# A graph-attention kernel in 64x64 array tiles: part of each softmax denominator summed on VectorE

## The chip, the cores and the metric

The kernel runs on one core of one Trainium2 chip. The metric is the device time of one execution in microseconds (us). The kernel before was run three times: 2678.79, 2678.89 and 2681.78 us, median 2678.89. The profiled execution took 2678.89 us; its span, from the first to the last recorded instruction, is 2677.1 us.

## The reference

One graph-attention layer with four heads, a second one with a single head on its output, then two layer normalisations with a residual. There are 8 batch entries, 2048 nodes and 64 features.

```python
mask = graph + eye(N) > 0                       # 2048 x 2048
h = einsum('bnc,hdc->bhnd', x, Wh)              # four heads of 64
# gat(h): scores = h h^T; where not mask: -1e16; softmax over m; times h; plus bias
z = leaky_relu(concat_heads(gat(h)), 0.2)
h2 = einsum('bnk,dk->bnd', z, Wo)
z2 = leaky_relu(gat(h2), 0.2)
out = layernorm(x + (layernorm(z2) * gamma + beta))
```

The softmax needs, for every query node, the sum over all 2048 nodes m of exp(score). These sums, the denominators, are what the change is about.

## The kernel before, in words

All times come from `fast_kernel`; `general_kernel` runs only if the range check at the end asks for it.

**Units, chunks, blocks.** A unit is a pair of maps that are worked on together, one on partitions 0 to 63 and one on 64 to 127: two heads of one batch entry (a first-layer unit, 16 in all), or the second layer of two batch entries (a second-layer unit, 4 in all). The units are numbered 0 to 19 in the order of the list `order`; 5, 10, 18 and 19 are of the second layer. A unit has 4 chunks of 512 query nodes, a chunk 16 blocks of 128 nodes m: 1280 steps, each one block of one chunk.

**One step** t. TensorE makes the scores of its block (`scores`, L537: 4 products in 64x64 array tiles, of which float32 makes 8 instructions) into one of two PSUM buffers "s" of 128x1024. VectorE subtracts the mask from them and writes the block's tile e, 128x1024 float32, to SBUF (L540). ScalarE takes the exponential in place (L541). Three steps later (`LAG`) TensorE multiplies e by the values (`values`, L550: again 8 instructions), and `add_up` deals with the denominator. On TensorE a step is thus scores of block t, then values of block t-3. The next scores but one need the same "s" buffer, so they wait for the subtraction.

**The denominator.** Before, blocks 1 to 12 of a first-layer chunk (1 to 8 in the second layer) are added into acc by GpSimd, one addition of 128x1024 each (L559 the first, L563 the others). The last blocks, 3 or 7 by `DIRECT`, stay as they are. With acc that makes 4 or 8 terms. `sums` (L597) has TensorE multiply each half of the terms by ones, in 128x32 tiles, four at a time: 2 or 4 groups of 8 instructions. The result goes by ScalarE (L600) and small DMAs to `invert` (L613, L615), which inverts it and sends it back by DMA, spread over partitions; `scale` (L624) multiplies.

**Order.** Every engine works its instructions in the order in which they are written. Jobs hang on a chunk's first step t (`LATE`, `NORM`): join at t+19, join2 (VectorE, L577) and sums at t+20, fifth t+21, leaky (VectorE, L585) t+22, invert t+24, scale t+28, project (TensorE, L641 in odd chunks of the second pair of heads, L631 in every second-layer chunk) t+30. A chunk's jobs from t+16 on so run among the blocks of the next chunk: "step 4 of the next chunk" is t+20. In the last chunk of a unit, steps 1 and 6 prepare the next unit (`prepare`: 8 transposes, L527, into an "s" buffer, which VectorE copies with an addition, L529). `NORM` are the second layer's normalisation parts from t+31 to t+46, on ScalarE, VectorE and GpSimd: at t+43 GpSimd takes a power (L694), which ScalarE needs at t+46 (L698). In the first 60 steps the byte mask is built beside the work.

**Buffers.** The tiles e, and raw pieces of adj and x, share 13 buffers of 4 KB ("e", `epool`); results of 512 columns share 6 ("w", `work`).

Of the kernel before, what the change touches and what calls it, by code (L numbers as in the profile page):

```python
# [24 lines left out]
F32 = mybir.dt.float32  # L29
# [4 lines left out]
OP = mybir.AluOpType  # L34
AX = mybir.AxisListType
# [320 lines left out]
def fast_kernel(ctx: ExitStack, tc: tile.TileContext, x, adj, Wh, bh, Wo, bo, gamma, beta, out, flag):  # L356

    nc = tc.nc
    B, N, C = x.shape
    H, D, _ = Wh.shape  # L360
    P = 128
    NB = N // P
    W = 512
# [2 lines left out]
    HP = H // 2  # L366
    K = 2 * CB
    LAG = 3
    DIRECT = (3, 7)

    const = ctx.enter_context(tc.tile_pool(name="const", bufs=1))
    big = ctx.enter_context(tc.tile_pool(name="big", bufs=2))
    epool = ctx.enter_context(tc.tile_pool(name="epool", bufs=13))
    accs = ctx.enter_context(tc.tile_pool(name="accs", bufs=2))
    work = ctx.enter_context(tc.tile_pool(name="work", bufs=6))
    small = ctx.enter_context(tc.tile_pool(name="small", bufs=4))
    psum = ctx.enter_context(tc.tile_pool(name="psum", bufs=2, space=bass.MemoryType.PSUM))
    dram = ctx.enter_context(tc.tile_pool(name="scratch", bufs=4, space=bass.MemoryType.DRAM))
# [1 line left out]
    def slot(shape, dtype, name):  # L380
        return epool.tile(shape, dtype, tag="e", name=name)

    def spsum(name, dtype=F32):
        n = 2 * W * 4 // mybir.dt.size(dtype)
        return psum.tile([P, n], dtype, tag="s", name=name)
# [4 lines left out]
    def wtile(name):  # L390
        return work.tile([P, W], F32, tag="w", name=name)
# [13 lines left out]
    for r in range(2):  # L405
        half = centre[r * D:(r + 1) * D, r, :]
        nc.vector.tensor_scalar(half, half, -1.0 / D, None, OP.add)
    ones = const.tile([P, 32], F32, name="ones")
# [20 lines left out]
    def load_x(bp):  # L429
        sts = []  # L430
        for h in range(2):
            st = slot([P, NB // 2, 2, C], F32, f"x{bp}_{h}")
            for b2 in range(2):
                nc.sync.dma_start(out=st[:, :, b2, :],
                                  in_=x[2 * bp + b2, h * N // 2:(h + 1) * N // 2].rearrange("(c p) d -> p c d", p=P))
            sts.append(st)
        return sts

    def transpose_x(bp, sts, h):
        if h == 0:  # L440
            xT[bp] = big.tile([P, N], F32, tag="xT", name=f"xT{bp}", bufs=1)
        p = spsum(f"px{bp}_{h}")
        for k in range(NB // 2):
            nc.tensor.transpose(p[:, k * P:(k + 1) * P], sts[h][:, k].rearrange("p b d -> p (b d)"), ident)
        nc.scalar.copy(xT[bp][:, h * 1024:(h + 1) * 1024], p)
# [52 lines left out]
    def project_x(bp, hp, q):  # L498

        if q == 0:  # L500
            maps[bp, hp] = big.tile([P, 2, N], F32, tag="hT", name=f"hT{bp}_{hp}")
        p = spsum(f"ph{bp}_{hp}_{q}").rearrange("p (b i) -> p b i", b=2)
        for b2 in range(2):
            rows = slice(b2 * C, (b2 + 1) * C)
            for j in range(2):
                nc.tensor.matmul(p[j * D:(j + 1) * D, b2, :], whT[rows, hp * P + j * D:hp * P + (j + 1) * D],
                                 xT[bp][rows, q * W:(q + 1) * W], start=True, stop=True)
        nc.scalar.copy(maps[bp, hp][:, :, q * W:(q + 1) * W], p)  # L508

    class Unit:  # L510
# [21 lines left out]
        def scores(self, c, m):  # L532
            ps = spsum(f"s{self.n}_{c}_{m}").rearrange("p (j i) -> p j i", j=2)
            for k in range(2):
                for j in range(2):
                    rows = slice(j * D, (j + 1) * D)
                    nc.tensor.matmul(ps[k * 64:(k + 1) * 64, j, :], self.hT[rows, m * P + k * 64:m * P + (k + 1) * 64],  # L537
                                     self.hT[rows, c * W:(c + 1) * W], start=True, stop=True)
            e = slot([P, 2, W], F32, f"e{self.n}_{c}_{m}")
            nc.vector.tensor_tensor(e, ps, mask[c][:, m, :].unsqueeze(1).to_broadcast([P, 2, W]), OP.subtract)  # L540
            nc.scalar.activation(e, e, AF.Exp, bias=shifts[:, 1:2] if self.second else shifts[:, 0:1], scale=1.0)  # L541
            return e
# [10 lines left out]
        def add_up(self, c, m, e):  # L553

            if m == 0:
                self.terms[c] = [e]
            elif m == 1:
                acc = accs.tile([P, 2, W], F32, tag="acc", name=f"acc{self.n}_{c}")
                nc.gpsimd.tensor_tensor(acc, self.terms[c][0], e, OP.add)  # L559
                self.terms[c] = [acc]  # L560
            elif m < NB - DIRECT[self.second]:
                acc = self.terms[c][0]
                nc.gpsimd.tensor_tensor(acc, acc, e, OP.add)  # L563
            else:
                self.terms[c].append(e)


        def join(self, c):
# [18 lines left out]
        def sums(self, c):  # L587

            n = self.n
            pz = spsum(f"pz{n}_{c}")  # L590
            terms = self.terms.pop(c)
            half = len(terms) // 2
            for k in range(half):
                for s in range(2):
                    for j in range(2):
                        q = (2 * s + j) * 32
                        nc.tensor.matmul(pz[q:q + 32, :W], ones, terms[s * half + k][:, j, :],  # L597
                                         start=(k == 0), stop=(k == half - 1), tile_position=(0, q))
            zsb = wtile(f"zsb{n}_{c}")
            nc.scalar.copy(zsb, pz[:, :W])  # L600
            zt = small.tile([P, 2, 8], F32, tag="zt", name=f"zt{n}_{c}")
            with nc.allow_non_contiguous_dma(reason="2 KB"):
                for s in range(2):
                    for j in range(2):
                        q = (2 * s + j) * 32
                        nc.sync.dma_start(out=zt[j * D:(j + 1) * D, s, :],
                                          in_=zsb[q:q + 1, :].rearrange("o (p k) -> o p k", k=8))
            self.zt[c] = zt

        def invert(self, c):  # L610
            n = self.n
            k = n * NC + c
            nc.vector.tensor_reduce(zall[:, k, :], self.zt.pop(c).rearrange("p s k -> p k s"), AX.X, OP.add)  # L613
            rt = small.tile([P, 8], F32, tag="rt", name=f"rt{n}_{c}")
            nc.vector.reciprocal(rt, zall[:, k, :])  # L615
            rd = dram.tile([2, W], F32, tag="rd", name=f"rd{n}_{c}")
            nc.sync.dma_start(out=rd.rearrange("j (p k) -> (j p) k", k=8), in_=rt)
            self.z[c] = wtile(f"z{n}_{c}")
            for j in range(2):
                nc.sync.dma_start(out=self.z[c][j * D:(j + 1) * D, :], in_=rd[j].partition_broadcast(D))  # L620

# [98 lines left out]
    def at(t, job):  # L720
        jobs.setdefault(t, []).append(job)
# [36 lines left out]
    for t in range(total + 64):  # L758
        if t < total:
            u, c, m = steps[t]  # L760
            es[t] = u.scores(c, m)
            if m == 0:
                for d, name in LATE:
                    at(t + d, lambda u=u, c=c, name=name: getattr(u, name)(c))
                for part, d in enumerate(NORM):
                    at(t + d, lambda u=u, c=c, part=part: u.norm(c, part))

                n = u.n + 1
                if n < len(units):
                    v = units[n]  # L770
                    lead = not v.second and v.b2 == 0
                    if lead and v.hp == 0:
                        if c == 0:
                            xst[v.bp] = load_x(v.bp)
                        elif c == 1:
                            for h in range(2):
                                at(t + 2 + 4 * h, lambda v=v, h=h: transpose_x(v.bp, xst[v.bp], h))
                    if lead and c == 2:
                        for q in range(NC):
                            at(t + 1 + 3 * q, lambda v=v, q=q: project_x(v.bp, v.hp, q))  # L780
                    if c == 3:
                        for h in range(2):
                            at(t + 1 + 5 * h, lambda v=v, h=h: v.prepare(h))
        if 0 <= t - LAG < total:
            u, c, m = steps[t - LAG]
            e = es.pop(t - LAG)
            u.values(c, m, e)
            u.add_up(c, m, e)
        for job in jobs.pop(t, ()):
            job()  # L790
# [53 lines left out]
```

## Time and profile before

| | |
|---|---|
| median of 3 runs | 2678.89 us |
| profiled execution | 2678.89 us, its span 2677.1 us |
| TensorE matmul busy | 2580.8 us (96%), 23174 instructions |
| VectorE busy | 1832.5 us (68%) |
| ScalarE busy | 1783.3 us (67%) |
| GpSimd busy | 2265.1 us (85%) |
| granted TensorE clock | 0.985 in the mean |
| scores L537, values L550 | 20480 matmul instructions of the 23174 |
| denominators on TensorE, L597 | 1536 matmul instructions |
| denominators on GpSimd, L559 and L563 | 896 additions of some 2.37 us |

In the page, PE is TensorE, DVE VectorE, ACT ScalarE, POOL GpSimd, SP the engine that issues most DMAs; L540 is line 540 of the kernel. Matmuls overlap, so a group of 8 that is listed with 1.04 us is followed by the next group 0.86 us after its start; where the distance matters, starts are compared and not durations. An idle time stands beside the engine's instruction that came after it, with what released it.

### The profile page before, as it was taken

To read this page: it belongs to the slowest core of one execution; us is meant where nothing else is said; L and a number is where in the kernel's file an instruction comes from. 1 tells how busy PE (TensorE), PEld (TensorE's weight loads), DVE (VectorE), ACT (ScalarE), POOL (GpSimd) and SP (SyncE) were. 2 spreads that over 40 slices of the span, in tenths; PEclk is the share of its full clock that TensorE was granted. 3 is DMA by queue.
4 is the path that set the end of the run, shared out by engine and by line. 5 is a ranking of instruction groups with operands and counts; after the bars stand their busy time and mean duration, and the time that the engine had idled before them with its cause. 6 is when DMAs were issued, how large, how long until landed. Compare 5 with 4: busy or idle time off the path is not lost.

```text
span 2677.1 us, 54824 instructions
## 1 busy us (share of the span) xinstructions
PE 2580.8 (96%) x23174; PEld 896.5 (33%) x23174; DVE 1832.5 (68%) x1797; ACT 1783.3 (67%) x2089; POOL 2265.1 (85%) x1041
## 2 busy tenths in 40 slices
PE   7999999999999999999999899999999999999993
PEld 3333333333333233333333233333333333333331
DVE  5876776677766577667776667767776777766662
ACT  5766666666667666666667766666666666666774
POOL 5889999899688999889967989988998999967774
PEclk9999999999999999999999999999999999999996
DMA  5300001000001001000001000100000000000011
GB/s 143 125 25 10 9 9 25 10 14 10 13 17 25 9 14 25 10 10 10 10 14 25 21 9 10 25 9 14 9 9 10 10 10 13 10 13 17 21 25 29
DMA packets 118304, 55.40 MB, mean 21 GB/s; under 512 B 91266, under 2 KB 107714, under 8 KB 118050
## 3 DMA queue, kind: packets, MB, share of 16 engines
q1 hardware_dynamic: 117250, 51.36, 7.2%
q8 instruction: 183, 3.00, 0.5%
q0 software_dynamic: 176, 0.26, 0.1%
q14 instruction: 71, 0.58, 0.1%
q10 hardware_dynamic: 624, 0.20, 0.0%
HBM read 46.60 MB, written 4.52 MB: 19 GB/s over the span
## 4 chain that ended last, share of the span: by engine, by line
PE 76%; POOL 11%; ACT 6%; DVE 3%; issue 3%; DMA 0%; SPq 0%; POOLq 0%; DVEq 0%; ACTq 0%
PE s L537 34%; PE o L550 33%; POOL acc L563 6%; PE pz L597 5%; ACT e L541 3%; DVE e L540 2%; PE pn L527 1%; ACT xr L698 1%; PE o L641 1%; ACT xr L690 1%; POOL acc L559 1%; POOL st L694 1%; POOL st L679 1%; ACT hT L508 1%; PE pm L484 1%
## 5 line engine op out<-in xcount | busy, mean ns | idle before, releaser
L540 DVE TENSOR_TENSOR e<-s,mask 128x1024 f32<-128x1024 f32 x1280 | 1562.6, 1222 | 721.7 <-PE s L537 700.3
L563 POOL TENSOR_TENSOR acc<-acc,e 128x1024 f32<-128x1024 f32 x816 | 1933.5, 2369 | 81.2 <-ACT e L541 20.2
L541 ACT ACTIVATE e<-e,shifts 128x1024 f32<-128x1024 f32 x1280 | 1465.1, 1148 | 762.5 <-DVE e L540 748.4
L550 PE MATMUL o<-e,hN 64*64 64x512 f32 x10240 | 1336.6, 592 | 20.2 <-ACT e L541 20.1
L537 PE MATMUL s<-hT 64*64 64x512 f32 x8192 | 1074.3, 595 | 9.6 <-DVE e L540 4.5
L550 PEld LDWEIGHTS o<-e,hN 64*64 64x64 f32 x10240 | 390.9, 134 | 738.6 <-issue 540.7
L537 PEld LDWEIGHTS s<-hT 64*64 64x64 f32 x8192 | 295.8, 133 | 582.2 <-issue 424.9
L559 POOL TENSOR_TENSOR acc<-e,e 128x1024 f32<-128x1024 f32 x80 | 189.3, 2367 | 139.5 <-ACT e L541 139.2
L537 PE MATMUL s<-h2T 64*64 64x512 f32 x2048 | 273.1, 604 | 15.7 <-DVE e L540 15.6
L597 PE MATMUL pz<-e,ones 128*32 128x512 f32 x1216 | 182.1, 600 | 0.0
L679 POOL TENSOR_TENSOR st<-st,mhalf 128x8 f32<-128x8 f32 x16 | 26.3, 1641 | 127.3 <-ACT st L678 127.3
L537 PEld LDWEIGHTS s<-h2T 64*64 64x64 f32 x2048 | 75.2, 135 | 157.9 <-issue 121.3
L597 PE MATMUL pz<-acc,ones 128*32 128x512 f32 x320 | 85.0, 610 | 0.1
L600 ACT COPY zsb<-pz 128x512 f32<-128x512 f32 x80 | 46.7, 584 | 48.3 <-PE pz L597 48.3
L698 ACT ACTIVATE xr<-y,st 128x64 f32<-128x64 f32 x128 | 44.1, 426 | 42.8 <-POOL st L695 42.8
L597 PEld LDWEIGHTS pz<-e,ones 128*32 128x32 f32 x1216 | 41.0, 110 | 68.5 <-issue 68.5
L585 DVE TENSOR_TENSOR o<-o,o 128x512 f32<-128x512 f32 x80 | 55.8, 698 | 5.2 <-ACT o L581 5.2
L624 DVE TENSOR_TENSOR z<-o,z 128x512 f32<-128x512 f32 x80 | 54.5, 681 | 6.0 <-DMA z<-rd 5.7
L577 DVE TENSOR_TENSOR o<-o,oj 128x512 f32<-128x512 f32 x80 | 55.9, 698 | 2.4 <-ACT oj L572 1.0
L485 DVE CAST mask<-pm 128x1024 uint8<-128x1024 bf16 x32 | 39.1, 1223 | 18.5 <-PE pm L484 16.6
L581 ACT ACTIVATE o<-o 128x512 f32<-128x512 f32 x80 | 46.2, 577 | 0.0
L572 ACT COPY oj<-o 128x512 f32<-128x512 f32 x80 | 45.6, 569 | 0.4
(74 smaller groups left out, 681.8 us busy)
## 6 DMA issues: line engine op xcount, KB each, us to landing
z<-rd SPq DMA_DIRECT2D x160, 128.0 KB, 2.9
adj<-in_adj_dram SPq DMA_DIRECT2D x32, 512.0 KB, 4.8
zt<-zsb SPq DMA_DIRECT2D x320, 2.0 KB, 1.8
x<-in_x_dram SPq DMA_DIRECT2D x16, 256.0 KB, 4.6
xr<-in_x_dram SPq DMA_DIRECT2D x32, 128.0 KB, 2.7
out_dram<-xr SPq DMA_DIRECT2D x32, 128.0 KB, 2.1
rd<-rt SPq DMA_DIRECT2D x80, 4.0 KB, 1.4
ws<-in_L_gnn_Wh_dram ACTq DMA_DIRECT2D x2, 64.0 KB, 4.6
```

The source lines that it names most:

```text
L537: nc.tensor.matmul(ps[k * 64:(k + 1) * 64, j, :], self.hT[rows, m * P + k * 64:m * P + (k + 1) * 64], self.hT[rows, c * W:(c + 1) * W], st ...
L540: nc.vector.tensor_tensor(e, ps, mask[c][:, m, :].unsqueeze(1).to_broadcast([P, 2, W]), OP.subtract)
L541: nc.scalar.activation(e, e, AF.Exp, bias=shifts[:, 1:2] if self.second else shifts[:, 0:1], scale=1.0)
L550: nc.tensor.matmul(self.O[c][r][j * D:(j + 1) * D, :], self.hN[rows, m, j * D:(j + 1) * D], e[rows, j, :], start=(m == 0), stop=(m == NB - 1))
L559: nc.gpsimd.tensor_tensor(acc, self.terms[c][0], e, OP.add)
L563: nc.gpsimd.tensor_tensor(acc, acc, e, OP.add)
L577: nc.vector.tensor_tensor(b, b, self.t, OP.add)
L585: nc.vector.tensor_tensor(b, b, self.t, OP.max)
L597: nc.tensor.matmul(pz[q:q + 32, :W], ones, terms[s * half + k][:, j, :], start=(k == 0), stop=(k == half - 1), tile_position=(0, q))
L624: nc.vector.tensor_tensor(dst, self.O[c][1], self.z[c], OP.mult)
L679: nc.gpsimd.tensor_tensor(st[:, 0, :], st[:, 1, :], mhalf, OP.pow)
L698: nc.scalar.activation(v(xr)[:, k, :], v(y)[:, k, :], AF.Identity, bias=st[:, 1, k:k + 1], scale=st[:, 0, k:k + 1])
```

## The change

Blocks 2, 4, 6 and 8 of every chunk are written into one tile, eb, with a single buffer. GpSimd no longer adds them; instead `reduce` has VectorE sum the four, in four instructions per chunk. Each reads one half of the query columns of one map in all four blocks (256 columns of 4 values, which lie 4 KB apart) and writes 256 columns of a tile part. They are issued at t+13, t+14, t+15 and t+17. `DIRECT` becomes (0, 4): GpSimd adds blocks 1, 3, 5, 7 and 9 to 15 in the first layer, 1, 3, 5, 7 and 9 to 11 in the second. The terms for `sums` are then 2 (acc and part) and 6 (acc, part and four blocks). The "e" buffers become 9, the "w" buffers 4; the tile z of `invert` gets two buffers of its own. Nothing else changes.

```diff
-    DIRECT = (3, 7)
+    BATCH = (2, 4, 6, 8)
+    DIRECT = (0, 4)
...
-    epool = ctx.enter_context(tc.tile_pool(name="epool", bufs=13))
+    epool = ctx.enter_context(tc.tile_pool(name="epool", bufs=9))
...
-    work = ctx.enter_context(tc.tile_pool(name="work", bufs=6))
+    work = ctx.enter_context(tc.tile_pool(name="work", bufs=4))
...
-            e = slot([P, 2, W], F32, f"e{self.n}_{c}_{m}")
+            if m == BATCH[0]:
+                self.eb = epool.tile([P, len(BATCH), 2, W], F32, tag="eb", name=f"eb{self.n}_{c}", bufs=1)
+            e = self.eb[:, BATCH.index(m)] if m in BATCH else slot([P, 2, W], F32, f"e{self.n}_{c}_{m}")
...
+            elif m in BATCH:
+                self.batch = self.eb
             elif m < NB - DIRECT[self.second]:
...
+        def reduce(self, c, k):
+
+            if k == 0:
+                self.part = []
+                self.terms[c].append(self.part)
+            j, i = k // 2, slice(k % 2 * 256, k % 2 * 256 + 256)
+            if k % 2 == 0:
+                self.part.append(wtile(f"part{self.n}_{c}_{j}"))
+            nc.vector.tensor_reduce(self.part[j][:, i], self.batch[:, :, j, i].rearrange("p k i -> p i k"), AX.X, OP.add)
...
+            pick = lambda term, j: term[j] if isinstance(term, list) else term[:, j, :]
...
-                        nc.tensor.matmul(pz[q:q + 32, :W], ones, terms[s * half + k][:, j, :],
+                        nc.tensor.matmul(pz[q:q + 32, :W], ones, pick(terms[s * half + k], j),
...
-            self.z[c] = wtile(f"z{n}_{c}")
+            self.z[c] = work.tile([P, W], F32, tag="z", name=f"z{n}_{c}", bufs=2)
...
+                for k, d in enumerate((13, 14, 15, 17)):
+                    at(t + d, lambda u=u, c=c, k=k: u.reduce(c, k))
```

## The prediction, made before the result was known

> **What bounds the kernel now.** I read the page first: the busy shares, the slices and the chain that ended last.
>
> ```profile
> span 2677.1 us, 54824 instructions
> ...
> PE 2580.8 (96%) x23174; PEld 896.5 (33%) x23174; DVE 1832.5 (68%) x1797; ACT 1783.3 (67%) x2089; POOL 2265.1 (85%) x1041
> ...
> PE   7999999999999999999999899999999999999993
> ...
> PE 76%; POOL 11%; ACT 6%; DVE 3%; issue 3%; DMA 0%; SPq 0%; POOLq 0%; DVEq 0%; ACTq 0%
> ```
>
> TensorE is full from the second slice to the last but one: a group of matmuls taken away is time saved, if nothing else comes late. GpSimd is next. Then the timeline of TensorE, VectorE and GpSimd in an ordinary first-layer chunk, which shows how much room each has.
>
> ```profile
> 1266.34 1.04 PE L550 MATMUL o<-e,hN 64*64 64x512 f32 x8
> 1267.20 1.04 PE L537 MATMUL s<-hT 64*64 64x512 f32 x8
> 1268.06 1.04 PE L550 MATMUL o<-e,hN 64*64 64x512 f32 x8
> ...
> 1270.88 1.09 PE L537 MATMUL s<-hT 64*64 64x512 f32 x8
> ```
>
> ```profile
> 1255.71 0.68 DVE L624 TENSOR_TENSOR z<-o,z 128x512 f32<-128x512 f32 x1
> 1256.31 1.21 DVE L540 TENSOR_TENSOR e<-s,mask 128x1024 f32<-128x1024 f32 x1
> ...
> 1268.37 1.22 DVE L540 TENSOR_TENSOR e<-s,mask 128x1024 f32<-128x1024 f32 x1 [0.49 <-PE s L537]
> ```
>
> ```profile
> 1238.67 26.87 POOL L563 TENSOR_TENSOR acc<-acc,e 128x1024 f32<-128x1024 f32 x11
> 1265.71 2.37 POOL L559 TENSOR_TENSOR acc<-e,e 128x1024 f32<-128x1024 f32 x1 [0.16 <-ACT e L541]
> ```
>
> Groups start 0.859 us apart, so a step lasts 1.717 us. An ordinary chunk lasts 29.48 us (starts of its first scores): 16 steps are 27.47, and the two groups of L597 with their edges 2.01. VectorE idles 0.49 us a step. GpSimd's additions start 2.44 apart (26.87/11): 12 take 29.3 of the 29.48, so it has no room, and what the normalisation adds makes it late. Last the waits, and TensorE's and GpSimd's timeline just after a second-layer unit:
>
> ```profile
> ACT xr L698 <- POOL st L695: 42.8, 13, 6.3
> ...
> PE o L550 <- ACT e L541: 20.1, 7, 4.9
> PE s L537 <- DVE e L540: 20.1, 10, 3.9
> ```
>
> ```profile
> 875.33 1.65 POOL L694 TENSOR_TENSOR st<-st,mhalf 128x8 f32<-128x8 f32 x1
> ```
>
> ```profile
> 881.14 1.56 PE L550 MATMUL o<-e,hN 64*64 64x512 f32 x8 [4.94 <-ACT e L541]
> ```
>
> GpSimd reaches the power L694 late, ScalarE waits for it in order (L698), the exponentials queue behind, and TensorE idles.
>
> **What the skill says.** "VectorE: DVE Perf Modes", section "The perf-mode tier table (the rule you actually need)": tensor_reduce runs at one element per cycle only. The trace agrees: 512 inputs (L675) take 685 ns, 640 (L795) 810, about 1 ns each. "Vector Engine (DVE) Microarchitecture Reference", section "5.2 Measured stream behaviour on trn2 (trn3 not measured)": a two-source operation with one source hopping 4 KiB at every element takes 1.73 ns per column, yet a one-source read that hops 16 KiB every element and writes one word per two reads keeps the full rate. No row of this trace hops 4 KB; L613 hops 32 bytes at every element and takes 159 ns for 16 inputs, where the full rate gives 810 - 624 x 1.04 = 161. "SBUF — State Buffer", section "Who interferes with whom": tensor_reduce never contends with GpSimd; nothing here shows it, since these reductions are few.
>
> **The change, part by part.**
>
> *TensorE.* Each chunk loses one group of 8 (2 groups become 1, 4 become 3): 80 x 0.859 = **68.7 us less**.
>
> *VectorE.* Four reductions of 1024 inputs per chunk. At full rate one takes 810 + 384 x 1.04 = 1210 ns; with the hop price, as an estimate by section 5.2, 1210 + 1024 x 0.69 = 1920. I take 1.21: the one-source case and L613 are nearer to it. Queued instructions start about 0.085 us before the one ahead ends (L624 above: 0.68 long, the next starts 0.60 on), so a subtraction occupies 1.14, a reduction 1.13. The room for being late: scores start, the subtraction starts 1.18 later and takes 1.22, the next scores but one start 3.43 after the first; where they waited, they started 0.055 after the subtraction's end. Room: 3.43 - 1.18 - 1.22 - 0.055 = **0.975 us**.
>
> Now the lateness of each subtraction. Subtraction and reduction are 1.14 + 1.13 - 1.717 = 0.55 more than a step; a step without one recovers 1.717 - 1.14 = 0.58. Block 12 is followed by scale (0.60): block 13 is 0.02 late, 14 0.57, 15 1.12, the next chunk's block 0 1.67, block 1 1.09, block 2 1.64 (the reduction at t+17), then it falls. The excess over 0.975 stops TensorE: 0.145 after block 15, 0.695 in all after block 0; block 2's 0.665 is covered by that. So an ordinary chunk stalls **0.70 us** for the 0.859 it saves. By chunk kind:
> - 39 chunks with neither project nor prepare near: 39 x 0.70 = 27.
> - 8 before a prepare, without project: the addition L529 stands behind the reduction at step 1. The subtraction of block 1 starts at 1.18 + 0.40 after its scores; 1.14, 1.13 and 1.22 later L529 ends, 5.07; the scores two steps on are due at 3.43 + 1.0 for the transposes = 4.43, and wait 0.055 more. Hence 0.70 + 0.69 = 1.39, x 8 = 11.
> - 8 of that kind with project at step 14: 2.03 us of TensorE work there (31.51 against 29.48) let VectorE catch up, 0.3 of the prepare stall stays: 2. 9 with project or its second-layer counterpart and no prepare: 0.
> - 16 second-layer chunks: VectorE waits for ScalarE's square there anyhow (L675: 46.8 us of idle time), which hides some; between 0 and 1.1 each, taken 0.4: 6.
> - Block 2 of each chunk writes eb behind the reduction that reads it, on the same engine. L615 after L613 starts 0.034 after its end rather than 0.085 before: 0.12 x 47 = 6.
>
> Sum on VectorE's account: **+52**.
>
> *GpSimd.* 11 additions for 12, 26.8 us per chunk; and ahead of L694 (step 11) stand 4 additions, not 8, so it comes at least 4 x 2.44 = 9.8 us earlier. Chunks that are longer than their kind add up to 55 us: unit 5's last 5.6, unit 6's first three 0.4, 4.0 and 9.2 (33.49 for 29.48, 43.07 for 33.88); the same in 10 and 11; 16.6 in 18 and 19. The longest wait for L695 is 6.3. Part of it is ScalarE's own eight instructions (2.8 to 4.2 us), and after L694 come 7 additions in a row (17.1 us) that can reach sums late where GpSimd starts a chunk late, about 3 us for units 6 and 11. I take **36 us less**, with 15 and 50 as ends. In an ordinary chunk the last addition ends some 0.5 us before sums needs it: nothing.
>
> *Start and buffers.* 9 "e" buffers for 12 tiles per chunk are enough (a tile lives up to 6 steps), but in the first 60 steps the raw adj pieces take 8 more, and "w" has 4 buffers with part held from t+13 to t+20. Three chunks, each 0 to 5 us: taken **+5** in all. New waits of ScalarE's queue elsewhere: none, since part is read before sums and o5 follows sums anyhow. SP's queue keeps its DMAs.
>
> Sum: -68.7 + 52 - 36 + 5 = -47. Against its own 2678.9 (span 2677.1 and 1.8 around it; the median of the runs is the same): **2632 us**.
>
> **The rivals.**
> - *B, GpSimd's relief doesn't come*: ScalarE's own normalisation work holds the exponentials, only 68.7 - 57 = 12 us are gained: 2667. For it: ScalarE is 67% busy in the mean and fuller in second-layer chunks. Against: the 42.8 us of L698's waits name GpSimd.
> - *C, the hop of 4 KB costs at every element* (slower). A reduction takes 1.92, occupies 1.83, and each adds 1.25 us of lateness: block 0 is 3.77 late, block 2 4.4, so an ordinary chunk stalls 3.5 instead of 0.70, +2.8. 47 such chunks: 132; 17 with project some 1.6: 27; 16 second-layer some 2: 32. 2632 + 191 = 2823. It decides from about 1.45 us per reduction: 0.24 more, four times, in the 47 chunks are 45, and the gain is gone. For it: the reads do hop 4 KB every time. Against: L613 and the one-source case.
> - *D, the change doesn't do what it says*: the four blocks in one tile are tracked as one, so that values of block 2 wait for block 4's exponential. That ends 1.18 + 1.22 + 0.035 + 1.15 = 3.6 us after its scores, while the values are due 2.58 after them: 1.08 with the hand-over, three times a chunk, 80 chunks, +259: 2891. No row of before shows a tile that two engines share block by block, so nothing excludes it; I only take it as unlikely.
>
> **How the numbers follow.** The forecast A has 0.62, B 0.18, C 0.16, D 0.04. A's own range: relief 50, no start cost, second-layer stalls 0 and no hand-over, 2632 - 14 - 5 - 6 - 6 = 2601; reductions of 1.30 us (+17), relief 15 (+21), start 15 (+10), 2680. With B inside, 2600 to 2685 leaves C and D out, 0.20. A difference of 0.2%, 5 us, is about what a measurement of this kernel can tell from none. Faster by more: A and nearly all of B, 0.77; within: 0.03; slower: C and D, 0.20.
>
> **What would show it.** The new row TENSOR_REDUCE part<-eb: 320 times, near 1210 ns (A) or 1900 (C). L597: 896 instructions. TensorE's listed wait for the subtraction, L537 <- L540, grows from 20 to some 40 us (a group is listed 0.18 us longer than its distance to the next, so a stall shows that much shorter), at steps 1 to 3 of a chunk; ordinary chunks last 29.3, those with project 30.65. ACT xr L698 <- POOL falls from 42.8 to under 10, and the third chunk of unit 6 from 43.1 to some 37. Wrong if the reductions take over 1.4 us, or if TensorE waits for GpSimd's acc at sums.

## The result, and the profile after

The changed kernel takes 2864.74 us (median of 4 runs, 2863.75 to 2865.22) against 2678.84 for the kernel before on the same chip: ratio 1.0691, 95% interval 1.0672 to 1.0709. It is 186 us slower. The forecast was 2632, its range 2600 to 2685; rival C had 2823.

From the page of the changed kernel, as before:

```profile
span 2862.5 us, 53599 instructions
...
PE 2566.9 (90%) x22534; PEld 851.8 (30%) x22534; DVE 2410.8 (84%) x2117; ACT 1771.7 (62%) x2089; POOL 2074.0 (72%) x961
...
PE 19%; DVE 15%; issue 4%; POOL 3%; ACT 2%; DMA 0%; DVEq 0%; SPq 0%; POOLq 0%; ACTq 0%
```

TensorE did its part: 640 instructions fewer. But it is busy for 90% of a longer span, no longer 96%, and VectorE has risen from 1832.5 to 2410.8 us and stands in the chain with 15%, where it had 3%. The chain's shares do not add up to the span here, so I read from them only which engine came in. The groups of VectorE say what rose:

```profile
L542 DVE TENSOR_TENSOR e<-s,mask 128x1024 f32<-128x1024 f32 x960 | 1165.8, 1220 | 265.4 <-PE s L537 248.1
...
L579 DVE TENSOR_REDUCE part<-eb 128x256 f32<-128x1024 f32 x320 | 637.0, 1991 | 0.0
```

A reduction takes 1991 ns, not 1210; it never waits for data (idle before it 0.0). The timeline of VectorE shows three of them with subtractions between, without a pause:

```profile
1083.91 2.00 DVE L579 TENSOR_REDUCE part<-eb 128x256 f32<-128x1024 f32 x1
1085.81 1.23 DVE L542 TENSOR_TENSOR e<-s,mask 128x1024 f32<-128x1024 f32 x1
1086.94 1.99 DVE L579 TENSOR_REDUCE part<-eb 128x256 f32<-128x1024 f32 x1
1088.84 1.23 DVE L542 TENSOR_TENSOR e<-s,mask 128x1024 f32<-128x1024 f32 x1
1089.97 2.00 DVE L579 TENSOR_REDUCE part<-eb 128x256 f32<-128x1024 f32 x1
```

Subtractions start 3.03 us apart there, where TensorE's step is 1.717. TensorE's timeline at the end of the chunk before, where the same thing happens, shows what that does, in square brackets the idle time and what ended it:

```profile
1057.52 1.09 PE L537 MATMUL s<-hT 64*64 64x512 f32 x8 [1.08 <-DVE e L542]
...
1060.56 1.09 PE L537 MATMUL s<-hT 64*64 64x512 f32 x8 [1.09 <-DVE e L542]
...
1064.92 1.09 PE L537 MATMUL s<-hT 64*64 64x512 f32 x8 [0.70 <-DVE eb L542]
```

An ordinary chunk lasts 32.6 us (29.48 before). And the waits, among them those that took the place of the one foretold to go. First one of the kernel before, then those of the changed kernel:

```profile
POOL st L694 <- ACT st L693: 9.6, 3, 4.5
```

```profile
PE s L537 <- DVE e L542: 127.5, 155, 2.4
...
POOL st L709 <- ACT st L708: 92.5, 16, 6.4
...
PE s L537 <- DVE eb L542: 46.7, 55, 1.5
...
PE pz L612 <- POOL acc L567: 16.0, 4, 5.3
...
ACT xr L713 <- POOL st L710: 4.1, 2, 2.0
```

Scores waited 20.1 us for the subtraction before, now 127.5 + 46.7. ScalarE's wait for GpSimd's power has fallen from 42.8 to 4.1 us, as forecast. But GpSimd, now early, waits for ScalarE before that power (L709 here, L694 before: from 9.6 to 92.5 us), and TensorE waits for acc at sums (L612), which the prediction had named as a sign of being wrong.

### The profile page after: what moved, and what is told of

It reads as the page before. It is cut to its first block, busy times and chain, and to the rows that moved or that the text cites. A ratio compares the mean times of both kernels' runs of the same rounds, so it can differ in the third digit from the quotient of the medians.

```text
span 2862.5 us, 53599 instructions
## 1 busy us (share of the span) xinstructions
PE 2566.9 (90%) x22534; PEld 851.8 (30%) x22534; DVE 2410.8 (84%) x2117; ACT 1771.7 (62%) x2089; POOL 2074.0 (72%) x961
## 5 line engine op out<-in xcount | busy, mean ns | idle before, releaser
L567 POOL TENSOR_TENSOR acc<-acc,e 128x1024 f32<-128x1024 f32 x736 | 1743.3, 2369 | 513.2 <-ACT e L543 477.6
L543 ACT ACTIVATE e<-e,shifts 128x1024 f32<-128x1024 f32 x960 | 1098.6, 1148 | 798.1 <-DVE e L542 796.4
L542 DVE TENSOR_TENSOR e<-s,mask 128x1024 f32<-128x1024 f32 x960 | 1165.8, 1220 | 265.4 <-PE s L537 248.1
L552 PE MATMUL o<-e,hN 64*64 64x512 f32 x7680 | 999.7, 591 | 1.9 <-ACT e L543 1.9
L579 DVE TENSOR_REDUCE part<-eb 128x256 f32<-128x1024 f32 x320 | 637.0, 1991 | 0.0
L543 ACT ACTIVATE eb<-eb,shifts 128x1024 f32<-128x1024 f32 x320 | 367.7, 1149 | 214.7 <-DVE eb L542 213.1
L542 DVE TENSOR_TENSOR eb<-s,mask 128x1024 f32<-128x1024 f32 x320 | 391.7, 1224 | 92.8 <-PE s L537 82.4
L552 PEld LDWEIGHTS o<-e,hN 64*64 64x64 f32 x7680 | 292.7, 133 | 537.7 <-issue 454.3
L552 PE MATMUL o<-eb,hN 64*64 64x512 f32 x2560 | 333.8, 592 | 0.0
L552 PEld LDWEIGHTS o<-eb,hN 64*64 64x64 f32 x2560 | 98.4, 134 | 179.3 <-issue 141.3
L612 PE MATMUL pz<-acc,ones 128*32 128x512 f32 x320 | 86.0, 616 | 16.1 <-POOL acc L567 16.0
L709 POOL TENSOR_TENSOR st<-st,mhalf 128x8 f32<-128x8 f32 x16 | 26.4, 1647 | 92.5 <-ACT st L708 92.5
L612 PE MATMUL pz<-part,ones 128*32 128x512 f32 x320 | 86.7, 614 | 0.6 <-DVE part L579 0.6
L694 POOL TENSOR_TENSOR st<-st,mhalf 128x8 f32<-128x8 f32 x16 | 26.4, 1648 | 68.9 <-ACT st L693 68.9
L615 ACT COPY zsb<-pz 128x512 f32<-128x512 f32 x80 | 45.9, 574 | 34.2 <-PE pz L612 34.2
```

Of the source, the lines that this page charges most:

```text
L552: nc.tensor.matmul(self.O[c][r][j * D:(j + 1) * D, :], self.hN[rows, m, j * D:(j + 1) * D], e[rows, j, :], start=(m == 0), stop=(m == NB - 1))
L579: nc.vector.tensor_reduce(self.part[j][:, i], self.batch[:, :, j, i].rearrange("p k i -> p i k"), AX.X, OP.add)
L612: nc.tensor.matmul(pz[q:q + 32, :W], ones, pick(terms[s * half + k], j), start=(k == 0), stop=(k == half - 1), tile_position=(0, q))
```

## The experiments

The theory after this, H: for each column VectorE reads one value from block 2, one from 4, one from 6 and one from 8, that order of reading makes a reduction dear, and dear reductions ahead of the subtractions stop TensorE. Rivals: it is the number and place of the extra instructions, or the smaller buffers (N); contention with other engines (called N too in the first price run); VectorE's total work, wherever it stands (Q). The text quoted with each run is what was expected before it ran; dots stand for lines of code or of a view that are not shown. All ratios are to the kernel before on the same chip, its medians 2681.2 to 2681.7 us.

**1. The same reductions, reading neighbours.**

```diff
-nc.vector.tensor_reduce(self.part[j][:, i], self.batch[:, :, j, i].rearrange("p k i -> p i k"), AX.X, OP.add)
+nc.vector.tensor_reduce(self.part[j][:, i], self.batch[:, k].rearrange("p j (i f) -> p (j i) f", f=4), AX.X, OP.add)
...
```

> The changed kernel, but each of the four reductions reads one whole block of eb (1024 neighbouring columns, four to a sum) in place of 256 columns of four blocks that lie 4 KB apart: as many instructions, inputs and outputs, at the same steps. It leaves out the right denominators: 1e30 is added to each, and the second layer's scores are multiplied by zero. Theory H (the read order makes the reduction dear, and a dear reduction ahead of the subtractions stops TensorE): a reduction falls from 1.99 to about 1.21 us, an ordinary chunk from 32.6 to 29.3-29.5 us, the whole to 2630-2655 us. Rival N (four more instructions of any kind in that place, or the smaller buffers, cost it): stays within 2% of 2865 us.

Measured: 2665.09 us, ratio 0.9938 (0.9922 to 0.9955). The group of this kernel, whose lines stand one further down:

```profile
L580 DVE TENSOR_REDUCE part<-eb 128x256 f32<-128x1024 f32 x320 | 386.8, 1209 | 0.0
```

As many instructions of the same shape at the same steps, in the order of memory: 1209 ns, 202 us less than the change by the ratios, and 0.6% less than the kernel before. N falls; the order of reading is the cause of the whole loss. (This kernel computes other sums; run 7, which has them all, shows the same.) The ordinary chunk takes 29.48 us; the prediction's count of lateness had 29.3 for this price. The total is 10 us over H's span and 33 over the forecast; most of the 33 is found in the next run.

**2. No reductions.**

```diff
-                self.part = []
-                self.terms[c].append(self.part)
...
-            nc.vector.tensor_reduce(self.part[j][:, i], self.batch[:, :, j, i].rearrange("p k i -> p i k"), AX.X, OP.add)
...
+                self.terms[c].append(self.terms[c][0])
...
```

> The changed kernel without the four reductions; acc takes part's place in the sums on TensorE, so the matmuls stay as many. It leaves the four blocks out of the denominators, adds 1e30 to each and multiplies the second layer's scores by zero. Theory H: everything that the change gives and nothing that it costs on VectorE: 2678.9 - 68.7 (TensorE) - 36 (GpSimd's relief) + 5 = 2579 us, ordinary chunks 28.6 us. Rival N, if the buffers are at fault: clearly over 2679.

Measured: 2603.32 us, ratio 0.9707 (0.9691 to 0.9724). So the change brings 78 us before anything that it costs on VectorE, not the 100 of the forecast. Most of the difference is after the second-layer units: the second and third chunk of unit 6 take 39.0 and 40.8 us (33.5 and 43.1 before; the prediction had some 37 for the third). GpSimd's and TensorE's timeline there:

```profile
814.43 1.65 POOL L703 TENSOR_TENSOR st<-st,mhalf 128x8 f32<-128x8 f32 x1 [4.42 <-ACT st L702]
...
816.32 14.58 POOL L568 TENSOR_TENSOR acc<-acc,e 128x1024 f32<-128x1024 f32 x6
```

```profile
835.98 1.94 PE L606 MATMUL pz<-acc,ones 128*32 128x512 f32 x8 [8.15 <-POOL acc L568]
...
873.61 1.94 PE L606 MATMUL pz<-acc,ones 128*32 128x512 f32 x8 [5.38 <-POOL acc L568]
```

GpSimd idles 4.4 us in front of the power, and the additions of blocks 9 to 15 are queued behind it. They now include the last blocks of the chunk, which the kernel before gave to TensorE directly, so sums has to wait for them: 8.2 and 5.4 us. Runs 9 and 10 test this.

**3. Plain additions in place of reductions.**

```diff
+            b = self.eb
+            if k < 2:
+                nc.vector.tensor_tensor(b[:, 2 * k], b[:, 2 * k], b[:, 2 * k + 1], OP.add)
+            else:
+                part = slot([P, 2, W], F32, f"part{self.n}_{c}")
+                nc.vector.tensor_tensor(part, b[:, 0], b[:, 2], OP.add)
+                self.terms[c].append(part)
...
-                for k, d in enumerate((13, 14, 15, 17)):
+                for k, d in enumerate((7, 11, 15)):
```

> The changed kernel with three plain additions of 128x1024 on VectorE in place of the four reductions: block 2 + block 4 at t+7, block 6 + block 8 at t+11, the two sums at t+15 into an e buffer. The same sums. Theory H: no hops and 3 x 1.22 us in place of 4 x 1.99, far enough apart that each is worked off (0.55 us late, 0.58 recovered per step): no stall, about 2580 us. Rival P (additions with two SBUF inputs collide with GpSimd's reads, as the Trainium skill's page SBUF - State Buffer, section Who interferes with whom, has it): an addition takes up to 1.2 + 2.4 us, or GpSimd's slow by as much, and the time lies between 2620 and 2750.

Measured: 2774.19 us, ratio 1.0343 (1.0325 to 1.0360). H's 2580 is wrong. P has the right mechanism, but the time lies 24 us above its span. The groups of this kernel on VectorE and GpSimd:

```profile
L574 DVE TENSOR_TENSOR eb<-eb 128x1024 f32<-128x1024 f32 x160 | 263.5, 1647 | 0.0
...
L577 DVE TENSOR_TENSOR part<-eb 128x1024 f32<-128x1024 f32 x80 | 218.7, 2734 | 0.0
```

```profile
L567 POOL TENSOR_TENSOR acc<-acc,e 128x1024 f32<-128x1024 f32 x736 | 1873.2, 2545 | 341.4 <-ACT e L543 300.7
```

The addition at t+15, where GpSimd adds nearly without a pause, takes 2734 ns in the mean; GpSimd's own rise from 2369 to 2545. Alone, an addition of this shape takes 1224 (next run). In this trace the 41 of the 240 additions during which GpSimd does nothing take 1212 to 1217 ns, the other 199 take 2173 in the mean and up to 3347: it is GpSimd's work beside them that makes them dear. That agrees with the section "Who interferes with whom" of the Trainium skill's page "SBUF — State Buffer": a VectorE instruction with two SBUF inputs contends with GpSimd's reads, a reduction does not. For reductions run 1 agrees too: 30 of its 320 met no work of GpSimd, and they took 1209 ns like the others. So the change's choice of a reduction had a reason.

**4. and 5. The prices alone.** The kernel before with more VectorE instructions at its end, three of each kind. A "place" below is a separate spot in memory from which one value is taken before the next is read elsewhere:

```diff
+        nc.vector.tensor_reduce(got[:, :256], flat[:, :1024].rearrange("p (i k) -> p i k", k=4), AX.X, OP.add)
+        nc.vector.tensor_reduce(got[:, :256], four[:, :, :256].rearrange("p k i -> p i k"), AX.X, OP.add)
+        nc.vector.tensor_reduce(got[:, :512], two[:, :, :512].rearrange("p k i -> p i k"), AX.X, OP.add)
...
```

> The kernel before with 30 more VectorE instructions at its end, when all else is done: the prices alone. Each three times: 1024 inputs to 256 sums, neighbouring (theory H: 1.21 us) and 4 KB apart (1.99); 512 sums of two 8 KB apart; 512 sums of two 32 bytes apart; 8, 4, 16 and 64 sums of few inputs, 32 bytes or 4 KB apart (H: 0.16 for 16 inputs 32 bytes apart; 16, 64, 256 inputs 4 KB apart show whether the price is per element from the first one on: 143 + 1.8 ns each = 172, 258, 604 ns); 128 sums of eight inputs that come in neighbouring pairs, pairs 4 KB apart (1.21 if the pair is what counts); and an addition of 128x1024 with both inputs in SBUF (1.22). Rival N: the 4 KB row is near 1.21 here and the 1.99 in the kernel is contention with the other engines.

> The kernel before with more VectorE reductions at its end, three of each. Four inputs per sum 32 bytes apart and 1 KB apart; three 4 KB apart; two 4 KB apart; eight 2 KB apart; four 4 KB apart whose columns are every second word. If the number of streams counts (more than two lose the neighbour in the meantime): four and three and eight are dear at any distance, 1.6-1.9 ns per input, two are at 1.04. If the distance counts: 32 bytes and 1 KB are cheap.

Measured, the groups of the first of these kernels: L810 four neighbours, L812 four 4 KB apart, L814 two 8 KB apart, L816 two 32 bytes apart, L818 the same with 16 inputs, L820 16 inputs, four 4 KB apart, L826 neighbouring pairs, L828 the addition.

```profile
L812 DVE TENSOR_REDUCE got<-z 128x256 f32<-128x1024 f32 x3 | 5.7, 1889 | 0.1
L814 DVE TENSOR_REDUCE got<-z 128x512 f32<-128x1024 f32 x3 | 3.7, 1231 | 0.1
L828 DVE TENSOR_TENSOR z<-z 128x1024 f32<-128x1024 f32 x3 | 3.7, 1224 | 0.1
L816 DVE TENSOR_REDUCE got<-z 128x512 f32<-128x1024 f32 x3 | 3.7, 1221 | 0.1
L810 DVE TENSOR_REDUCE got<-z 128x256 f32<-128x1024 f32 x3 | 3.7, 1220 | 0.1
L826 DVE TENSOR_REDUCE got<-z 128x128 f32<-128x1024 f32 x3 | 3.7, 1220 | 0.1
...
L820 DVE TENSOR_REDUCE got<-z 128x4 f32<-128x16 f32 x3 | 0.5, 178 | 0.1
L818 DVE TENSOR_REDUCE got<-z 128x8 f32<-128x16 f32 x3 | 0.5, 170 | 0.1
```

And of the second: L808 four 32 bytes apart, L810 four 1 KB apart, L816 eight 2 KB apart, L812 three 4 KB apart (1008 inputs), L814 two 4 KB apart.

```profile
L808 DVE TENSOR_REDUCE got<-z 128x256 f32<-128x1024 f32 x3 | 5.9, 1966 | 0.1
...
L810 DVE TENSOR_REDUCE got<-z 128x256 f32<-128x1024 f32 x3 | 5.7, 1885 | 0.1
L816 DVE TENSOR_REDUCE got<-z 128x128 f32<-128x1024 f32 x3 | 5.6, 1871 | 0.1
L812 DVE TENSOR_REDUCE got<-z 128x336 f32<-128x1008 f32 x3 | 3.9, 1307 | 0.1
L814 DVE TENSOR_REDUCE got<-z 128x512 f32<-128x1024 f32 x3 | 3.7, 1231 | 0.1
```

Four places are dear alone on the engine (1889), so contention is not the main cause. Distance hardly counts: two inputs 32 bytes, 4 KB or 8 KB apart cost 1221 to 1231 ns, four cost 1885 to 1966 at 32 bytes, 1 KB and 4 KB. What counts is how many places are read in turn, one value from each: two at the full rate, three nearly (1307, where the second text had them among the dear), four and eight at some 1.7 ns per input. Four places with a pair of neighbours read from each are at the full rate (1220). The price is there from the first inputs on: with four places 4 KB apart, 16, 64 and 256 inputs took 178, 259 and 585 ns, where the first text had 172, 258 and 604. In the kernel the same reduction takes 1991, 0.10 more than alone. GpSimd explains little of that: the 13 of the 320 reductions that met no work of GpSimd took 1960. The rest stays open.

**6. The reductions further apart.**

```diff
-                for k, d in enumerate((13, 14, 15, 17)):
+                for k, d in enumerate((9, 11, 14, 17)):
```

> The changed kernel with its four reductions at t+9, t+11, t+14 and t+17 in place of t+13, 14, 15 and 17: as dear, but with time between them to catch up. Theory H (a queue with 0.975 us of room): each makes 1.33 us of lateness, of which 0.58 per step is recovered; an ordinary chunk 30.9 in place of 32.6 us, one with project 32.2 for 34.3, in all some 2785 us. Rival Q (the total of VectorE's work counts, not where it stands): stays at 2865 us.

Measured: 2791.82 us, ratio 1.0413 (1.0397 to 1.0429), with 1986 ns a reduction; ordinary chunks 31.1 us, those with project 33.1. H had 2785, with 30.9 and 32.2 for the two kinds of chunk. Instructions as dear, moved by a few steps, give back some 74 of the 186 us: not the total of VectorE's work but the room in front of the subtractions decides. Q falls.

**7. Two blocks at a time.**

```diff
+            if k < 4:
+                b, out = self.eb[:, 2 * h:2 * h + 2, j], self.pair[j][:, h]
+            else:
...
+                b, out = self.pair[j], wtile(f"part{self.n}_{c}_{j}")
...
+            nc.vector.tensor_reduce(out, b.rearrange("p k i -> p i k"), AX.X, OP.add)
...
-                for k, d in enumerate((13, 14, 15, 17)):
+                for k, d in enumerate((7, 9, 11, 13, 15, 17)):
```

> The changed kernel with the same sums made two blocks at a time: six reductions of 1024 inputs (blocks 2 and 4 at t+7 and t+9, 6 and 8 at t+11 and t+13, the two pair sums at t+15 and t+17), the pair sums in two e buffers. Theory H (two streams read in turn keep the full rate, four do not): 1.21 us each, ordinary chunks 29.2 us, 2640-2660 us in all, faster than the kernel before although two more reductions are made. Rival Q (VectorE's total work counts: 6 x 1.21 = 7.3 us a chunk is nearly the 4 x 1.99 = 8.0 of the change): 2800 or more. Rival R (the e buffers are too few once two are held): over 2680.

Measured: 2673.95 us, ratio 0.9974 (0.9965 to 0.9983). Six reductions of 1238 ns, 7.4 us a chunk, in place of four of 1991, 8.0 us, and some 192 us less: H again, against Q. R falls too, since the time is under 2680. The ordinary chunk is 29.2 us as expected. But the total is 14 us over the span given; the second and third chunk after unit 5, and after unit 10, still last 41.0 and 41.1 us, where GpSimd is late.

**8. Thirteen e buffers.**

```diff
-    epool = ctx.enter_context(tc.tile_pool(name="epool", bufs=9))
+    epool = ctx.enter_context(tc.tile_pool(name="epool", bufs=13))
...
+            e = slot([P, 2, W], F32, f"e{self.n}_{c}_{m}")
...
```

> The kernel without reductions once more, but blocks 2, 4, 6 and 8 go into ordinary e buffers, of which there are 13 again: the same memory. Leaves out what that kernel leaves out (the four blocks in the denominators, 1e30 added to each, second-layer scores times zero). If the 9 buffers hold things up where GpSimd is late (VectorE's subtraction waited 54 us for GpSimd's additions there): 2585-2595 us, the third chunk after a second-layer unit under 40 us. If only GpSimd's late acc at sums counts: 2603 us as before.

Measured: 2606.17 us, ratio 0.9722 (0.9707 to 0.9736), against 0.9707 with 9. The wait of the subtraction for GpSimd has left the list, and nothing is gained: TensorE still waits 29.6 us for acc at sums. Having 9 e buffers and eb in place of 13 costs nothing; that wait had stood beside another. The four "w" buffers in place of six were not tried apart.

**9. and 10. Other blocks for VectorE.**

```diff
-    BATCH = (2, 4, 6, 8)
+    BATCH = (3, 6, 9, 11)
```

> The kernel without reductions once more, with blocks 3, 6, 9 and 11 left out of GpSimd's additions in place of 2, 4, 6 and 8. Leaves out what that kernel leaves out (four blocks in the denominators, 1e30 added to each, second-layer scores times zero). GpSimd makes as many additions, but 5 and not 7 of them stand behind the power at step 11, which waits 4 to 5 us for ScalarE after a second-layer unit. Theory G (GpSimd's relief was lost there: the additions behind the waiting power reach sums late, where TensorE waited 8.2 and 5.4 us): the two chunks after units 5 and 10 end some 5 us sooner each, ordinary chunks lose the last 0.13 us, in all 2603 to 2580-2590 us. Rival S (GpSimd has too much to do there, whatever the order): 2600 us or more.

Measured: 2576.13 us, ratio 0.9607 (0.9591 to 0.9623). The second and third chunk after unit 5 take 35.6 and 34.2 us in place of 39.0 and 40.8, ordinary ones 28.62. The time is 4 us below G's span. Its waits at sums:

```profile
PE pz L606 <- POOL acc L568: 9.0, 5, 3.8
```

It was 29.6 us with blocks 2, 4, 6 and 8. GpSimd makes as many additions, only their order differs: theory G holds, S falls. The same idea in the kernel that sums two by two:

```diff
-    BATCH = (2, 4, 6, 8)
+    BATCH = (3, 5, 7, 9)
```

> The kernel that sums two blocks at a time, with blocks 3, 5, 7 and 9 in place of 2, 4, 6 and 8; the same results. 6 additions stand behind the power at step 11, not 7. Theory G: 2.4 us sooner in each of the four chunks after units 5 and 10, and a little in ordinary ones: 2674 to 2660-2668 us. Rival S: 2674 us.

Measured: 2656.04 us, ratio 0.9907 (0.9891 to 0.9924), all sums computed: 0.9% less than the kernel before, and less than the changed kernel. It is again 4 us below G's span; the second and third chunk after unit 5 take 37.3 and 36.8 us in place of 41.0 and 41.1.

## Why the prediction was wrong, point by point

On the kernel before's 2679 us, the runs split the 186 us by differences of ratios: no reductions 0.9707 - 1, so -78; four reductions at the full rate 0.9938 - 0.9707, +62; reading four places in turn 1.0691 - 0.9938, +202. The sum is +186. The forecast had -100, +52 and nothing for the third.

- **The price of a reduction: the step that failed.** "I take 1.21: the one-source case and L613 are nearer to it." It is 1991 ns, and that is the +202 us. Both witnesses read only two places in turn, and two are free. The one-source case of section 5.2 in the Trainium skill's "Vector Engine (DVE) Microarchitecture Reference" is a stream that alternates between two regions; I wrote it down as a hop at every element and lost the two. The runs agree with it (1231 ns for two places, 8 KB apart) and with L613, but neither bears on four. L613 was doubly weak: with 16 inputs, two and four places differ by 8 ns (170 and 178). The same section's price of 1.73 ns per column for a two-source operation with one source hopping at every element, which I set aside, is near the 1.04 + (1889 - 1220)/1024 = 1.69 ns measured.
- **The room of 0.975 us and the count of lateness** held. Ordinary chunks: 29.3 forecast for 1.21, measured 29.48 in the run with that price; 30.9 for the spread reductions, measured 31.1; and with 1.99 the same count makes block 2 of the next chunk 0.02 + 4 x 1.33 - 0.58 = 4.76 us late, 3.8 over the room, so 28.6 + 3.8 = 32.4 for the change, measured 32.6. Chunks with project were put wrong: 30.65 forecast, 31.5 in run 1; 32.2 for the spread reductions, 33.1. Most of a stall falls at the start of the next chunk, so that with project keeps the stall that it inherits, and the one after it is spared: 28.6 us in run 1, as in run 2 without reductions.
- **VectorE's account at the full rate**: +52 forecast, +62 measured. 8.5 us of it fall in unit 0 (147.7 against 139.2 us of its four chunks, with and without reductions), where the mask is built beside them; I had counted those chunks like others, at 0.70 each.
- **TensorE's 68.7 us** came: 640 instructions fewer. **GpSimd's relief** was mis-sized, the second step that failed: -36 forecast. With the start's +5 the gains should have been 100 and were 78, so that, if the start cost the 5, the relief was some 14 (an estimate). The power no longer holds ScalarE (42.8 to 4.1 us), as foretold, but GpSimd now waits there for ScalarE, and the additions behind it delay sums by 8.2 and 5.4 us where I had put "about 3 us for units 6 and 11". With other blocks the gain is 105, so the relief was there to be had and the order of GpSimd's additions lost it. "In an ordinary chunk the last addition ends some 0.5 us before sums needs it" was also short: without stalls on VectorE a chunk takes 28.75 with blocks 2, 4, 6, 8 and 28.62 with 3, 6, 9, 11.
- **Start and buffers**: 13 "e" buffers changed nothing; the +5 for the start was not measured apart.
- **Rival B** fell: with other blocks the relief comes. That its 2667 is close to run 1 is luck: some 14 us more relief against 10 us more on VectorE's account. **Rival D** fell: TensorE never idles before the values of eb in the changed kernel (the line below), and in 316 of the 320 blocks they follow the scores after 0.86 or 0.91 us. **Rival C** was right in its price, 1.92 us as an estimate against 1.99, and in what it costs, +191 against 202. Its 2823 is 42 short: beside these 11 us it kept the forecast's other terms, with some 22 too much gain and 10 too little on VectorE. Its mechanism, the hop of 4 KB, was wrong: the distance hardly counts, the number of places does. That 1.92 came so near is in part luck, since 0.10 of the 1.99 has no known cause. Its point of decision, 1.45 us, was too high: a straight line between 1.21 us (17 us gained) and 1.99 us (186 lost) crosses zero at about 1.27, an estimate.

```profile
L552 PE MATMUL o<-eb,hN 64*64 64x512 f32 x2560 | 333.8, 592 | 0.0
```

So I had both prices from the start, chose the wrong one and gave the right one 0.16. A range that took in both would have been the honest one: nothing in the trace of before read four places in turn.

## What to carry to other kernels

An example stands for a case only where it has the same structure: before pricing a strided read, count how many places it takes in turn, one value from each, and use rows that take as many and are long enough to show it. An engine with a third of its time idle can still have no room in a queue that others wait for: count lateness step by step against the time to the next wait. And an engine that becomes early begins to wait for others in its own queue; what stands behind that wait should not be what the bound engine needs next.

## What the runs showed of the hardware

- A VectorE reduction of 1024 float32 values takes 1.22 to 1.23 us when its inputs come as neighbours, as pairs, or from two places in turn at 32 bytes, 4 KB and 8 KB; 1.87 to 1.97 when single values come from four or eight places, and 1.31 for 1008 values from three (runs 4 and 5). In the kernel, four places took 1.99.
- An addition of 128x1024 on VectorE with both inputs in SBUF took 1.22 us while GpSimd was idle and 2.17 in the mean, at most 3.35, while it worked; GpSimd's additions slowed from 2.37 to 2.55 in the mean (run 3). Reductions at the full rate, with one input, took 1.21 us with and without GpSimd's work (run 1).
